# The FFN's output bias row: added onto each block of x by an accumulating DMA in place of a GpSimd operation

## Chip, cores and metric

The kernel runs on one core of a Trainium2 chip. The metric is device time in microseconds (us), the median of several runs. Before the change it is 741.25 us (3 runs, 739.79 to 741.45).

## What is computed

The input x has shape 8 x 1024 x 256. It passes through one attention layer and one feed-forward layer, each added onto its input and normalised afterwards. Cut to what matters:

```python
q, k, v = x @ Wq.T + bq, x @ Wk.T + bk, x @ Wv.T + bv      # 16 heads of 16
q, k = softmax(q, over the 16 of a head), softmax(k, over the 1024 rows)
state = einsum('bhnd,bhne->bhde', k, v)
out = einsum('bhnd,bhde->bhne', q, state)
x = layernorm(x + (layernorm(out) * ln_g + ln_b) @ Wo.T + bo)

h = layernorm(x) * ln1_g + ln1_b
h = gelu(h @ ternary(w1).T + b1)                           # 1024 hidden
h = layernorm(h) * ln2_g + ln2_b
x = layernorm(x + h @ ternary(w2).T + b2)
```

## The kernel before

**Tiling.** A batch of 1024 rows lies in SBUF as 128 partitions by 8 tiles by 256 columns (`xs[b]`). It is worked in two blocks of 4 tiles, 16 blocks in all; `x_of(i)` is the view of block i, 128 x 1024 numbers. x stays in SBUF and is updated in place: each block receives its attention result, is normalised, is read by the FFN, receives the FFN's result, is normalised again and is sent out.

**Attention.** The main loop (L781) goes over the 16 blocks and two more. For a block it makes keys (`keys`, L311, with `keys_exp`, L329, which takes running maxima, L333 and L335, and then the exponential, L338), queries (`queries_max`, L375, whose subtraction L378 is GpSimd's, and `queries_sum`, L385, with L391 on GpSimd), and the products of keys and x (`keys_x`, L407). Then a DMA issued from GpSimd's queue adds a row `crow` onto the block's x (L855). Two blocks later `attend` (L486) applies the state. A generator `norm` (L514) takes the statistics of a batch, adds the attention output to x (L526) and derives the scales, with the reciprocal square root in small steps of VectorE (`rsqrt`, L115 to L132). Its steps are handed out a few at a time by `more(n)` at fixed places of the loop, so VectorE's order is fixed when the kernel is built. The application of the scale (L772) is ScalarE's.

**FFN.** `ffn_slots` (L720) is a second generator, in slots of one column group; 8 slots make a block. Each slot makes one half of a hidden tile (`hidden`, L597, matmuls L615 and L619, gelu L620), turns hidden values (`turn`, L636, transposes L643, copies L568 on ScalarE and L569 on VectorE), and multiplies by the second weight matrix (`product`, L648, L657). Hidden work leads the products by 11 slots. Every eighth slot calls `enter` (L571) for the next block: GpSimd makes the scaled copy `h0` of x (L576), which is turned into the FFN's input (`turn_input`, L592), and then it adds the row `bout` onto x in place (L579). `bout` is a row of 256 numbers, the same in all partitions, made once from b2, ln2_b and w2 (L247). Later in the block's own 8 slots VectorE adds the part of the mean (`add_mean`, L680), then the FFN's result times its scale (`outputs`, L716), and takes statistics (`result_stats`, L686). One block later `finish` (L663) lets GpSimd scale and shift the four tiles (L670) and SP send them out (L673).

The FFN starts inside the attention loop: `enter(0)` runs at the last attention block but one, and three more calls of `enter` fall while the last attention blocks are still worked on. From block 4 on the FFN is alone. The order on each engine is that of the program (a manual schedule); semaphores between engines are set by the framework. An operation that reads or writes x waits for those before it that touch the same part.

**On GpSimd's queue**, therefore, stand in this order at each `enter`: the multiplication L576, the addition L579, and behind them whatever comes next: L378 and L391 of the next attention block with its L855, the next L576, or the four L670 of a finished block.

Of the kernel before, what the change touches and what calls it, by code (L numbers as in the profile page):

```python
# [12 lines left out]
ALU = mybir.AluOpType  # L13
AX = mybir.AxisListType

P = 128
# [6 lines left out]
def attn_ffn_postln_kernel(  # L23
# [11 lines left out]
    nc = tc.nc  # L35
    B, N, C = x.shape
# [6 lines left out]
    G = 4  # L43
# [96 lines left out]
    bout = const.tile([P, C], F32, name="bout")  # L140
# [152 lines left out]
    def x_of(i):  # L293
        b, g = blocks[i]
        return xs[b][:, g * G : (g + 1) * G, :]
# [275 lines left out]
    def enter(i):  # L571

        b, g = blocks[i]
        h0[i] = big.tile([P, G, C], F32, tag="h0", bufs=2, name=f"h0_{i}")
        rs2 = rs2_all[:, b * NT + g * G : b * NT + (g + 1) * G]
        nc.gpsimd.tensor_tensor(  # L576
            h0[i], x_of(i), rs2.unsqueeze(2).to_broadcast([P, G, C]), ALU.mult
        )
        nc.gpsimd.tensor_tensor(  # L579
            x_of(i), x_of(i), bout.unsqueeze(1).to_broadcast([P, G, C]), ALU.add  # L580
        )

    def turn_input(i, k):
# [136 lines left out]
    def ffn_slots():  # L720
        enter(0)
        yield
        turn_input(0, 0)
        turn_input(0, 1)
        for s in range(-LEAD, SLOTS):
            yield
            m = s + LEAD
            if m < SLOTS:
                if m % HC == 0 and m // HC + 1 < len(blocks):
                    enter(m // HC + 1)  # L730
                hidden(m)
                if m % HC in (5, 6) and m // HC + 1 < len(blocks):
                    turn_input(m // HC + 1, m % HC - 5)
            if 0 <= s + 2 < SLOTS:
                turn(s + 2)
            if m % 2 == 0 and 2 <= m < SLOTS + 2:
                squares((m - 2) // HC, (m - 2) % HC // 2)
            if s >= 0:
                norms(s)
                product(s)  # L740
                if s % HC == HC - 1:
                    outputs(s // HC)
        norms(SLOTS)
        norms(SLOTS + 1)
        last = len(blocks) - 1
        v = small.tile([P, 2 * NT], F32, tag="nv", name="nv_last")[:, :G]
        nc.vector.tensor_scalar(v, mv[last + 1][:, :G, 1], EPS, None, ALU.add)
        finish(last, mv[last + 1][:, :G, 0], finish_all(rsqrt(v, "last")))
# [167 lines left out]
```

## Time and profile before

| what | us |
|---|---|
| median of 3 runs | 741.25 (739.79 to 741.45) |
| profiled execution, its own time | 739.53 |
| span of its instructions | 737.8 |
| busy: TensorE matmuls | 690.7 (94% of the span) |
| busy: TensorE weight loads (beside matmuls) | 549.1 (74%) |
| busy: VectorE | 583.7 (79%) |
| busy: ScalarE | 441.0 (60%) |
| busy: GpSimd | 194.8 (26%) |

The profile is of one execution. PE is TensorE, PEld its weight loads, DVE VectorE, ACT ScalarE, POOL GpSimd, SP the engine that issues output DMAs. L579 is line 579 of the kernel; a group or a timeline line names line, engine, operation, what is written and read, the shape and the count; a bracket at its end tells how long the engine had been idle and who released it. In a timeline the first two numbers are start and duration in us. In the view of stretches a line gives the stretch, its length, busy time with the number of instructions for PE, PEld, DVE, ACT and POOL, then the clock granted to TensorE (1.00 is full), the DMA engines' share and GB/s. In the view of one source line durations are ns, as least, median and most. The page's mean clock over the span is 0.978.

### The profile page before, as it was taken

How to read it: one execution, taken by the hardware profiler on the slowest of the kernel's cores; microseconds unless marked ns; L12 is line 12 of the kernel's file. 1: busy time of each engine (PE TensorE's matmuls, PEld its weight loads, DVE VectorE, ACT ScalarE, POOL GpSimd, SP SyncE). 2: the span in 40 equal slices, each digit the busy share in tenths (PEclk: the TensorE clock that was granted, in tenths of full speed). 3: DMA queues.
4: the chain of work that ended last, by engine and by line, in shares of the span. 5: the costliest groups of instructions: out<-in, count | busy, mean ns of one | idle time of the engine just before them, and what ended most of it. 6: DMA issues, size and time to landing. Idle time of an engine off the chain costs nothing.

```text
span 737.8 us, 10770 instructions
## 1 busy us (share of the span) xinstructions
PE 690.7 (94%) x3780; PEld 549.1 (74%) x3780; DVE 583.7 (79%) x1642; ACT 441.0 (60%) x970; POOL 194.8 (26%) x156
## 2 busy tenths in 40 slices
PE   6899999979989999997998899999999999999992
PEld 4677766757657777765767788888888888888882
DVE  1667798877988959797898778877878877887686
ACT  2344436535364545546787667777777677677760
POOL 1232223121221222244420033332133333123112
PEclk9999999989999999998999899999999999999997
DMA  8833103222120111210100000000000000000001
GB/s 328 306 72 58 29 15 72 51 36 51 21 33 13 29 29 28 30 24 11 24 0 2 1 29 30 30 29 30 1 29 30 28 29 30 2 28 29 30 30 58
DMA packets 17238, 32.03 MB, mean 43 GB/s; under 512 B 1344, under 2 KB 12608, under 8 KB 16288
## 3 DMA queue, kind: packets, MB, share of 16 engines
q0 software_dynamic: 8608, 8.79, 7.9%
q1 hardware_dynamic: 7344, 21.50, 7.7%
q10 hardware_dynamic: 1232, 1.06, 0.4%
q8 instruction: 30, 0.49, 0.3%
q14 instruction: 24, 0.20, 0.1%
HBM read 14.56 MB, written 8.39 MB: 31 GB/s over the span
## 4 chain that ended last, share of the span: by engine, by line
PE 70%; DVE 23%; ACT 3%; DMA 2%; issue 2%; POOL 0%; POOLq 0%; ACTq 0%; DVEq 0%
PE pf L657 16%; PE ph L615 14%; PE pt L643 7%; PE po L498 6%; PE pq L364 5%; PE pa L407 5%; PE pk L322 5%; PE ph L619 3%; DVE x L526 3%; DVE st_y L532 2%; DMA wqkv_sb<-in_wqkv_dram 2%; PE pth L592 2%; PE ptq L301 1%; PE ptx L301 1%; DVE sto L508 1%
## 5 line engine op out<-in xcount | busy, mean ns | idle before, releaser
L657 PE MATMUL pf<-t,u 128*128 128x256 f32 x1024 | 157.5, 295 | 4.0 <-DVE x L716 3.6
L615 PE MATMUL ph<-t,hT 128*128 128x512 f32 x512 | 144.2, 403 | 1.2 <-DVE hT L569 1.2
L657 PEld LDWEIGHTS pf<-t,u 128*128 128x128 f32 x1024 | 131.9, 191 | 9.8 <-issue 5.8
L569 DVE SCALAR_TENSOR_TENSOR u<-pt,cols_sb,u 128x512 fp32r<-128x512 f32 x128 | 95.5, 746 | 45.6 <-ACT u L568 44.2
L620 ACT ACTIVATE h<-ph 128x512 f32<-128x512 f32 x128 | 76.5, 598 | 83.9 <-PE ph L619 73.7
L670 POOL TENSOR_SCALAR x<-x,ny_f,sh 128x256 f32<-128x256 f32 x60 | 38.1, 650 | 261.0 <-DVE sh L667 261.0
L615 PEld LDWEIGHTS ph<-t,hT 128*128 128x128 f32 x512 | 88.6, 189 | 15.3 <-DVE hT L569 1.9
L498 PE MATMUL po<-sm,qT 128*128 128x384 f32 x256 | 97.3, 505 | 0.1
L568 ACT ACTIVATE u<-pt,cols_sb 128x512 fp32r<-128x512 f32 x128 | 87.5, 684 | 8.3 <-PE pt L643 7.6
L643 PE MATMUL pt<-ident,h 128*128 128x128 f32 x512 | 78.1, 275 | 4.2 <-DVE u L569 2.5
L632 ACT ACTIVATE sq<-h,mvh 128x1024 f32<-128x1024 f32 x64 | 73.8, 1153 | 5.5 <-DVE mvh L624 5.5
L643 PEld LDWEIGHTS pt<-ident,h 128*128 128x128 f32 x512 | 61.6, 141 | 19.9 <-DVE hT L569 6.0
L378 POOL TENSOR_TENSOR q<-q,qm 128x1024 f32<-128x1024 f32 x16 | 30.8, 1926 | 150.1 <-DVE qm L377 90.6
L364 PE MATMUL pq<-wqkv_sb,xT 128*128 128x256 f32 x256 | 60.6, 380 | 0.8 <-DMA wqkv_sb<-in_wqkv_dram 0.8
L322 PE MATMUL pk<-xT,wqkv_sb 128*128 128x512 f32 x128 | 61.3, 603 | 0.0
L407 PE MATMUL pa<-x,ek 128*128 128x256 f32 x256 | 61.1, 382 | 0.0
L498 PEld LDWEIGHTS po<-sm,qT 128*128 128x128 f32 x256 | 46.5, 198 | 19.4 <-issue 2.1
L391 POOL TENSOR_TENSOR q<-q,rq 128x1024 f32<-128x1024 f32 x16 | 30.9, 1933 | 108.2 <-DVE rq L390 59.0
L407 PEld LDWEIGHTS pa<-x,ek 128*128 128x128 f32 x256 | 48.9, 192 | 13.1 <-issue 0.6
L364 PEld LDWEIGHTS pq<-wqkv_sb,xT 128*128 128x128 f32 x256 | 47.9, 190 | 12.7 <-issue 3.1
L680 DVE SCALAR_TENSOR_TENSOR x<-g2sum,ms,x 128x256 f32<-128x256 f32 x64 | 56.9, 927 | 0.0
L338 ACT ACTIVATE ekT<-pk,nb 128x512 f32<-128x512 f32 x32 | 21.7, 682 | 56.5 <-DVE nt_y L127 35.6
(144 smaller groups left out, 1151.9 us busy)
## 6 DMA issues: line engine op xcount, KB each, us to landing
x<-crow POOLq DMA_DIRECT2D x16, 512.0 KB, 5.5
out_dram<-x SPq DMA_DIRECT2D x16, 512.0 KB, 2.6
x<-in_x_dram SPq DMA_DIRECT2D x7, 1024.0 KB, 10.2
x<-in_x_dram SPq DMA_DIRECT2D x2, 512.0 KB, 5.6
wm_w<-in_w_dram SPq DMA_DIRECT2D x4, 256.0 KB, 8.0
wq_w<-in_w_dram SPq DMA_DIRECT2D x4, 256.0 KB, 2.5
wm_w<-in_w_dram SPq DMA_DIRECT2D x8, 128.0 KB, 2.1
wq_w<-in_w_dram SPq DMA_DIRECT2D x8, 128.0 KB, 2.0
```

The source lines that it names most:

```text
L322: nc.tensor.matmul(pk, wqkv_sb[:, k, C + c * P : C + (c + 1) * P], xT[i][:, k, :], start=(k == 0), stop=(k == KC - 1),)
L364: nc.tensor.matmul(pq[:, n, :], xT[i][:, k, (t + n) * P : (t + n + 1) * P], wqkv_sb[:, k, 0:C], start=(k == 0), stop=(k == KC - 1),)
L407: nc.tensor.matmul(pa[i][:, c, :], ek[i][:, t, c * P : (c + 1) * P], x_of(i)[:, t, :], start=(t == 0), stop=(t == G - 1),)
L498: nc.tensor.matmul(po[:, c * P : c * P + P + C], qT[i][:, c, t * P : (t + 1) * P], sm[b][:, c, :], start=(c == 0), stop=(c == KC - 1), ski ...
L568: nc.scalar.activation(hi, src, AF.Copy, scale=gain)
L569: nc.vector.scalar_tensor_tensor(lo, src, gain, hi.bitcast(F32), ALU.mult, ALU.subtract)
L615: nc.tensor.matmul(ph, hT[i][s][:, k, t * P : (t + 1) * P], t1[:, k, cols_j], start=(s == 0 and k == 0), stop=False,)
L620: nc.scalar.activation(h[i][t][:, cols_j], ph, AF.Gelu, accum_out=h[i, t][:, half : half + 1])
L632: nc.scalar.activation(sq, h[i][t], AF.Square, bias=mv[i][:, G + t, 0:1], accum_out=mv[i][:, G + t, 1:2])
L643: nc.tensor.transpose(pt[:, t * P : (t + 1) * P], h[i][t][:, j * P : (j + 1) * P], ident)
L657: nc.tensor.matmul(pf[i][t // 2][:, t % 2, :], u[s][:, n, t * P : (t + 1) * P], t2[:, j, :], start=(j == 0 and t % 2 == 0 and n == 0), sto ...
L680: nc.vector.scalar_tensor_tensor(x_t, g2sum, ms[i][:, t : t + 1], x_t, ALU.mult, ALU.add)
```

## The change

In `enter`, the GpSimd operation that adds `bout` onto the block is replaced by a DMA, issued from the same queue at the same place, that reads `bout` (repeated for the four tiles) and adds it onto x where x lies. Nothing else is changed.

```diff
         nc.gpsimd.tensor_tensor(
             h0[i], x_of(i), rs2.unsqueeze(2).to_broadcast([P, G, C]), ALU.mult
         )
-        nc.gpsimd.tensor_tensor(
-            x_of(i), x_of(i), bout.unsqueeze(1).to_broadcast([P, G, C]), ALU.add
+        nc.gpsimd.dma_start(
+            x_of(i), bout.unsqueeze(1).to_broadcast([P, G, C]), accum_op=ALU.add
         )
```

With it the waits change: the DMA waits for L576 on its own engine and for an earlier DMA that used the same semaphore; the first L680 of a block, its first L670 and its output DMA L673 now wait also for this DMA's landing. The order of instructions on every engine stays as it was.

## The prediction

> **What bounds the kernel now.** I looked first at what TensorE waits for in the pure FFN stage, 425 to 700 us, then at the operation that goes, then at every place where something near it is stretched. In the FFN stage TensorE waits for nobody: the view of waits is empty for it, and a stretch of 22 us, one block, is full. The line is stretch, length, then busy time of PE, weight loads, DVE, ACT and POOL.
>
> ```profile
> 512.00:534.00 22.00, 21.97 (x147) 19.27 (x146) 17.85 (x47) 15.95 (x35) 7.04 (x7) 1.00 0.07 26
> ```
>
> The operation is L579, 16 times, 2.46 us each. An accumulating DMA of the same shape is in the kernel already (L855, the row crow): 1.3 us on POOL, and the lines of the DMA view give 5.5 us to landing.
>
> ```profile
> L579 POOL TENSOR_TENSOR x<-x,bout x16: 2337/2463/2467, 330.9 to 669.4; 128x1024 f32<-128x1024 f32 x16
> L855 POOL DMA_DIRECT2D x<-crow x16: 1285/1298/1377, 30.1 to 347.9; - x16
> ```
>
> ```profile
> x<-crow POOLq DMA_DIRECT2D x16, 512.0 KB, 5.5
> ```
>
> Four of the 16 lie before 373 us, where attention and FFN overlap. There the timeline shows what L579 does to VectorE:
>
> ```profile
> 327.77 3.10 DVE L122 TENSOR_SCALAR ny_y<-nvy 128x16 int32<-128x16 int32 x1
> 328.39 2.44 POOL L576 TENSOR_TENSOR h<-x,rs_all 128x1024 f32<-128x1024 f32 x1
> ...
> 330.78 1.28 DVE L326 TENSOR_REDUCE mx<-pk 128x1 f32<-128x512 f32 x2
> 330.90 2.34 POOL L579 TENSOR_TENSOR x<-x,bout 128x1024 f32<-128x1024 f32 x1
> 332.09 1.17 DVE L333 TENSOR_TENSOR mb<-mx,bkv 128x2 f32<-128x2 f32 x1
> ...
> 333.55 0.69 ACT L338 ACTIVATE ekT<-pk,nb 128x512 f32<-128x512 f32 x1 [9.72 <-DVE nt_y L127]
> ...
> 334.38 0.47 PE L351 MATMUL pte<-ident,ekT 128*128 128x128 f32 x1 [3.50 <-ACT ekT L338]
> ```
>
> L333 writes two numbers a partition; its median is 161 ns, here it takes 1.17 us and ends at 333.26, when L579 ends (333.24). Likewise L122 ends with L576. Behind L333 wait the exponential of the keys and then TensorE, idle for 3.50 us. The chain of waits runs through exactly these: L122, L326, L333, L338, L351. The idle time has a second cost (the column before the DMA share is the granted clock):
>
> ```profile
> 331.00:333.00 2.00, 0.00 (x0) 0.00 (x0) 1.97 (x3) 0.00 (x0) 2.00 (x1) 1.00 0.94 134
> 333.00:334.00 1.00, 0.00 (x0) 0.00 (x0) 0.90 (x6) 0.45 (x1) 0.24 (x1) 0.98 0.00 0
> 334.00:340.00 6.00, 5.43 (x16) 3.80 (x17) 5.22 (x18) 3.45 (x11) 0.79 (x1) 0.50 0.00 1
> ```
>
> So TensorE works at half clock after the stall, until 340.8 us. A second run of stretched DVE steps:
>
> ```profile
> 352.42 1.19 DVE L519 TENSOR_SCALAR nvo<-mvo 128x8 f32<-128x8 f32 x1
> ...
> 353.64 1.82 DVE L122 TENSOR_SCALAR ny_o<-nvo 128x8 int32<-128x8 int32 x1
> 355.49 0.17 DVE L124 TENSOR_SCALAR ny_o<-ny_o 128x8 int32<-128x8 int32 x1
> 355.70 2.21 DVE L127 TENSOR_TENSOR nt_o<-ny_o 128x8 f32<-128x8 f32 x1
> 357.94 0.17 DVE L129 SCALAR_TENSOR_TENSOR nt_o<-nt_o,nvo 128x8 f32<-128x8 f32 x1
> ```
>
> POOL runs L579 from 351.20 to 353.57, L576 to 355.42, L579 from 355.50 to 357.88: L519, L122 and L127 each end with one of them.
>
> [...] The ends above agree to 0.04 us. During the issue of L855 at 288.54 us, L122 took 0.17 us: an issue alone did not hold it. [...] Half clock here lasts 6.83 us, two windows.
>
> **The change part by part.** The 16 L579 leave POOL; 16 issues of 1.3 us take their place in its queue, which keeps its order.
>
> At 330.9 us (block 0): L576 still ends at 330.83, so L122 keeps its 3.10 us. L333 starts at 332.09 and takes 0.16 instead of 1.17: 1.0 us less. The next operation on POOL comes only at 339.21[...]. L335, L338 and L351 follow, and TensorE's gap shrinks from 3.50 to 2.5 us. That is on the path: -1.0 us.
>
> The clock: by the trace, windows of 3.41 us in which TensorE was busy 0.10 to 0.32 of the time halved the clock, those at 0.49 and above did not (of 0.46 and 0.47 one of each). I lay such windows in every phase over a gap, close the gate where one is idle over 55%, and open it after a full busy one. A gap of 3.50 us then closes it in 93% of the phases and costs 2.0 us on average, 2.5 us in 63% and 1.2 us. The difference, about 0.85 us, is an estimate; in one execution it is 0 to 1.7. Bounds: at worst the restarted work falls wholly into half clock and 0.2 us are lost.
>
> At 351.2 us (blocks 1 and 2): the issue is followed at once by L576 of block 2, as L855 and L576 are at 347.89. That pair took until 351.12, 3.23 us; [...] from 351.2 to 354.4. L519 ends there, 0.9 us later than now, but L122 and L127 are free: L129 starts at 355.3 instead of 357.94, a lead of 2.6 us. The lead goes at two places. L624 at 358.62 needs ACT's accumulator, read out by 357.14, so 1.4 us remain; the L624 at 364.41 needs the one read out by 364.13, whose matmuls run on a TensorE without gaps: 0.2 us remain. At 368.41 L576 of block 3, which stays, blocks L526 as before, so TensorE's wait of 1.03 us at 371.24 stays too. I take -0.1 us; bounds 0 and -1.2 us (that wait and the 0.16 behind it).
>
> At 370.57 us (block 3) no DVE step is held by L579: 0.
>
> The other 12, every 21.9 us from 428.8 to 669.4: L579 stretches the second pair of L680 (3.14 us from 537.69, against 0.93 for the pair before). Up to 2.2 us of DVE time a block are freed, worth nothing: DVE afterwards waits for ACT's u (0.40 us) before the last L569 ahead of L716, and TensorE is never kept by the pair. If TensorE had slack, it would be worth at most 2.2 us a block.
>
> Added waits: the issue waits for L576 on its own engine, as L579 did, and for an old DMA on its semaphore, landed tens of us before. Behind it in POOL's queue are L378, L576 and L670; the issue is 1.1 us shorter than L579. The first L680 of a block, the first L670 and SP's output DMA wait for the landing. L680 of block 0 is at 398.99, 68 us after the issue, and 23 slots (63 us) follow for the others; 5.5 us are hidden. If the cover were gone, each block would pay 5.5 us. The last issue is 68 us before the end, so the tail is untouched.
>
> Sum: -1.0 - 0.1 - 0.85 = -1.95 us. The profiled execution took 739.53 us (span 737.8 and 1.7 around it), so 737.6; it lies 1.72 us under the median of the runs, 741.25, and from that I get 739.3.
>
> **The rivals.** Forecast, 0.50: 739.3; by the luck of the gate 738.4 to 740.2.
> The lead survives, 0.15: the steps between 352 and 372 take all of 1.2 us more: 741.25 - 3.15 = 738.1. For it speaks that DVE is busy 8.9 of 10 us there; against it the two waits for ACT and the L576 at 368.41.
> The gate gives nothing, 0.23: it falls as often and 0.2 us of the gain are lost: 741.25 - 1.1 + 0.2 = 740.35. For it: 2.5 us is still most of a window.
> Slower, 0.12: the 12 transfers in the stage that TensorE bounds slow its matmuls. A transfer of crow shows packets for 3.24 us; 12 make 38.9 us. Slowed by 5% they eat the 1.95 us; at 10% they cost 3.9 and the time is 743.2. For it: the four L615 within such a burst average 414 ns against 400 outside. Against it: L364, L322 and L498 have the same medians inside and outside bursts (379, 592, 486 ns), and L615's median too (395 and 396).
> That the change does not do what it says is excluded: the order of the instructions shows 16 copies of DMA in place of L579, and TensorE's and ACT's unchanged.
>
> **How the numbers follow.** What a measurement of this kernel can tell from no change is 0.2%, 1.5 us: 739.8. Of the forecast some 0.45 lies below it; with the second case 0.60. The third and the rest of the first are within, 0.28; slower 0.12. The low end, 737.2, is the second case with the gate's best luck (-1.1 - 1.2 - 1.7); the high end, 741.6, is past the third case by the scatter of the runs (741.45 at the highest). The slower case stays outside.
>
> **What would show it.** L333's longest near 0.16 us; TensorE's gap at 331 us about 2.5 us; less or no half clock after it; L127 at 0.17; L680's mean from 927 towards 550 ns; the wait before 371 us unchanged; a block still 21.9 us long. I am wrong if blocks lengthen, if L333 is still held[...], or if the gap at 371 closes.

## The result, and the profile after

The changed kernel takes 737.09 us (median of 22 runs, 734.84 to 739.95). The kernel before, run beside it on the same chip, takes 739.87 us (22 runs). The ratio is 0.9964 with a 95% interval of 0.9951 to 0.9977: 2.7 us less, between 1.7 and 3.6. The forecast was 739.3 us, 1.95 us below its median of before, 741.25 us; the ratio carried over to that median gives 738.6 us. What was gained is somewhat more than forecast, close to the rival "the lead survives" (3.15 us). The profiled execution took 737.86 us, with a span of 736.2.

In the view of one source line (least, median and most in ns) L333 is never held any more, L579 has become an issue of 1.3 us, and L680 has lost its long cases; its most was 2620 ns. The DMA view gives 5.5 us from issue to landing.

```profile
L333 DVE TENSOR_TENSOR mb<-mx,bkv x16: 160/160/163, 13.2 to 334.2; 128x2 f32<-128x2 f32 x16
```

```profile
L579 POOL DMA_DIRECT2D x<-bout x16: 1297/1304/1322, 333.2 to 667.8; - x16
```

```profile
L680 DVE SCALAR_TENSOR_TENSOR x<-g2sum,ms,x x64: 468/480/761, 396.9 to 723.5; 128x256 f32<-128x256 f32 x64
```

```profile
x<-bout POOLq DMA_DIRECT2D x16, 512.0 KB, 5.5
```

The timeline of the changed kernel at block 0:

```profile
329.83 3.10 DVE L122 TENSOR_SCALAR ny_y<-nvy 128x16 int32<-128x16 int32 x1
330.45 2.44 POOL L576 TENSOR_TENSOR h<-x,rs_all 128x1024 f32<-128x1024 f32 x1
...
333.19 1.31 POOL L579 DMA_DIRECT2D x<-bout  x1 [0.30 <-POOL h L576]
334.15 0.16 DVE L333 TENSOR_TENSOR mb<-mx,bkv 128x2 f32<-128x2 f32 x1
...
335.44 0.33 PE L351 MATMUL pte<-ident,ekT 128*128 128x128 f32 x1 [2.49 <-ACT ekT L338]
```

L122 is held by L576 exactly as long as before; L333, in the midst of the issue, is not; TensorE's gap is 2.49 us. The stretches after the gap (the clock is third from the end) still show half clock, but for one window of 3.41 us, where the profile of before had two:

```profile
335.40:336.70 1.30, 0.92 (x5) 0.72 (x6) 1.20 (x7) 0.66 (x2) 0.00 (x0) 1.00 1.20 173
336.70:340.10 3.40, 3.40 (x11) 2.20 (x10) 2.76 (x10) 2.07 (x7) 0.00 (x0) 0.51 0.52 76
340.10:342.00 1.90, 1.90 (x9) 1.34 (x9) 1.86 (x3) 1.08 (x3) 1.63 (x1) 0.98 0.00 0
```

A block of the FFN stage has TensorE as full as before, with VectorE 2 us less busy (15.85 us against 17.85):

```profile
512.00:534.00 22.00, 21.98 (x147) 19.20 (x146) 15.85 (x46) 15.77 (x36) 5.83 (x7) 1.00 0.22 48
```

The steps of the norm, from the timeline between 351 and 356 us. L519 alone is held, until L576 ends (2.28 us), and L129 follows at 355.29:

```profile
351.37 1.30 POOL L579 DMA_DIRECT2D x<-bout  x1 [0.30 <-POOL h L576]
352.19 2.41 POOL L576 TENSOR_TENSOR h<-x,rs_all 128x1024 f32<-128x1024 f32 x1
352.36 2.28 DVE L519 TENSOR_SCALAR nvo<-mvo 128x8 f32<-128x8 f32 x1
354.67 0.17 DVE L122 TENSOR_SCALAR ny_o<-nvo 128x8 int32<-128x8 int32 x1
...
355.09 0.17 DVE L127 TENSOR_TENSOR nt_o<-ny_o 128x8 f32<-128x8 f32 x1
355.29 0.17 DVE L129 SCALAR_TENSOR_TENSOR nt_o<-nt_o,nvo 128x8 f32<-128x8 f32 x1
```

Here the forecast fails. TensorE's wait at 371 us is gone. Before, the line was

```profile
372.27 0.50 PE L615 MATMUL ph<-t,hT 128*128 128x512 f32 x1 [1.03 <-DVE hT L569]
```

and no matmul of the changed kernel between 366 and 390 us waits.

**Where the 2.7 us come from.** To see it I set the start of every TensorE matmul in the profile after against the start of the same matmul in the profile before. The two executions already differ by +2.07 us when they reach 328 us, ahead of anything that was changed: 3.41 us of half clock from 22.72 us on, which the profile of before lacks, give +1.5 us, and half clock of 6.83 us in both, from 162.67 us on after and 159.88 us before, gives +0.6 us. From there on the difference moves like this:

| where (time in before) | step, us | what it is |
|---|---|---|
| 334 (L351) | -1.01 | the gap, 3.50 to 2.49 |
| 334 to 342 | -1.11 | half clock for 3.41 us in place of 6.83 |
| 361 | -0.37 | a wait of TensorE for y (L504), gone |
| 369 to 377 | -1.69 | the wait of 1.03 us for hT, its 0.16 us, and what followed |
| 409 to 426 | -0.4 | half clock at 409 us for 3.41 us in place of 6.83, at the same gap of 2.52 us: nothing near it was changed |
| 510 to 690 | +0.77 | 0.04 to 0.09 us a block, once 0.24 us |

The two profiled executions as a whole differ by only 1.67 us, since the 2.07 us of the start count against the change. Leaving out what the clock does, the steps are -1.01 - 0.37 - 1.69 + 0.77 = -2.3 us. So one item of the forecast is right, one much too small, and one was not in it at all: blocks of the FFN-only stage became longer.

### The profile page after: what moved, and what is told of

Its sections match the earlier page's. It is cut to its first block, busy times and chain, and to the rows that moved or that the text cites. A ratio compares the mean times of both kernels' runs of the same rounds, so it can differ in the third digit from the quotient of the medians.

```text
span 736.2 us, 10803 instructions
## 1 busy us (share of the span) xinstructions
PE 690.2 (94%) x3780; PEld 548.9 (75%) x3780; DVE 556.3 (76%) x1642; ACT 441.6 (60%) x970; POOL 177.0 (24%) x156
## 4 chain that ended last, share of the span: by engine, by line
PE 63%; DVE 19%; issue 9%; ACT 4%; DMA 3%; POOL 2%; ACTq 0%; POOLq 0%; DVEq 0%
PE ph L615 12%; PE pf L657 12%; PE po L498 7%; PE pt L643 5%; PE pa L407 5%; PE pq L364 5%; PE pk L322 5%; PE ph L619 3%; DMA wo_sb<-in_wo_dram 3%; DVE x L526 2%; DVE st_y L532 2%; POOL x L670 2%; PE ptq L301 1%; PE pth L592 1%; PE ptx L301 1%
## 5 line engine op out<-in xcount | busy, mean ns | idle before, releaser
L569 DVE SCALAR_TENSOR_TENSOR u<-pt,cols_sb,u 128x512 fp32r<-128x512 f32 x128 | 95.6, 747 | 66.0 <-ACT u L568 64.3
L615 PE MATMUL ph<-t,hT 128*128 128x512 f32 x512 | 143.7, 402 | 0.0
L620 ACT ACTIVATE h<-ph 128x512 f32<-128x512 f32 x128 | 76.6, 598 | 84.6 <-PE ph L619 74.3
L670 POOL TENSOR_SCALAR x<-x,ny_f,sh 128x256 f32<-128x256 f32 x60 | 38.5, 652 | 270.9 <-DVE sh L667 270.9
L615 PEld LDWEIGHTS ph<-t,hT 128*128 128x128 f32 x512 | 88.7, 189 | 13.6
L643 PE MATMUL pt<-ident,h 128*128 128x128 f32 x512 | 77.8, 274 | 4.7 <-DVE u L569 2.6
L643 PEld LDWEIGHTS pt<-ident,h 128*128 128x128 f32 x512 | 61.3, 140 | 21.2 <-DVE hT L569 7.0
L407 PE MATMUL pa<-x,ek 128*128 128x256 f32 x256 | 63.2, 392 | 0.0
L407 PEld LDWEIGHTS pa<-x,ek 128*128 128x128 f32 x256 | 50.5, 198 | 13.5 <-issue 0.6
L619 PE MATMUL ph<-brow,ones_r 128*128 128x512 f32 x128 | 50.7, 396 | 0.0
```

What stands on the lines that cost most here:

```text
L407: nc.tensor.matmul(pa[i][:, c, :], ek[i][:, t, c * P : (c + 1) * P], x_of(i)[:, t, :], start=(t == 0), stop=(t == G - 1),)
L569: nc.vector.scalar_tensor_tensor(lo, src, gain, hi.bitcast(F32), ALU.mult, ALU.subtract)
L615: nc.tensor.matmul(ph, hT[i][s][:, k, t * P : (t + 1) * P], t1[:, k, cols_j], start=(s == 0 and k == 0), stop=False,)
L619: nc.tensor.matmul(ph, ones_r, brow[:, cols_j], start=False, stop=True)
L620: nc.scalar.activation(h[i][t][:, cols_j], ph, AF.Gelu, accum_out=h[i, t][:, half : half + 1])
L643: nc.tensor.transpose(pt[:, t * P : (t + 1) * P], h[i][t][:, j * P : (j + 1) * P], ident)
```

## The experiments

Theory when I began: the first three DMAs give everything, through two separate places (block 0 through L333, blocks 1 and 2 through the norm's steps); the other twelve cost 0.8 us, because of a new wait on VectorE. Rivals: one place gives it all; the transfers themselves slow the blocks. All edits but that of "Later, with the GpSimd addition" are made in the changed kernel. "Before" is the kernel before on the same chip in the same series: 739.52 us (72 runs) for the first four, 739.56 (15) for the next four, 740.75 (11) for the rest.

### The DMA at block 0 alone

```diff
-        nc.gpsimd.dma_start(
-            x_of(i), bout.unsqueeze(1).to_broadcast([P, G, C]), accum_op=ALU.add
-        )
+        if i == 0:
+            nc.gpsimd.dma_start(
+                x_of(i), bout.unsqueeze(1).to_broadcast([P, G, C]), accum_op=ALU.add
+            )
+        else:
+            nc.gpsimd.tensor_tensor(
+                x_of(i), x_of(i), bout.unsqueeze(1).to_broadcast([P, G, C]), ALU.add
+            )
```

> Only block 0 is added by the DMA; the other 15 keep GpSimd's operation. Theory (L579 holds VectorE's steps in two places, each worth its own piece): L333 takes 0.16 us, TensorE's gap ahead of L351 (at 331 us before) is 2.5 us instead of 3.5, L127 in the stretch 352 to 358 us is still held (2.2 us), TensorE's wait for hT at 371 us is still 1.0 us, a lone FFN block lasts 21.87 us. Time against before: -1.0 us and 0 to -1.7 by the clock, so about -1.8. Rival (all of the gain hangs on the first gap, the rest follows from it): the wait at 371 us goes too and the time is about that of the full change, -2.8.

Measured: 738.97 us, ratio 0.9991 (0.998 to 1.0002). From its trace's timeline (lines after 579 stand five lower; L620 is L615):

```profile
333.46 0.16 DVE L333 TENSOR_TENSOR mb<-mx,bkv 128x2 f32<-128x2 f32 x1
...
334.75 0.33 PE L351 MATMUL pte<-ident,ekT 128*128 128x128 f32 x1 [2.50 <-ACT ekT L338]
...
354.95 2.21 DVE L127 TENSOR_TENSOR nt_o<-ny_o 128x8 f32<-128x8 f32 x1
...
371.52 0.49 PE L620 MATMUL ph<-t,hT 128*128 128x512 f32 x1 [1.02 <-DVE hT L569]
```

The gap shrinks, the norm's steps are held as ever, and the wait for hT stays. The trace confirms the place. The time is 0.5 us lower, 1.5 at most, and the interval just reaches no change at all: 1.0 us of gap fits, 1.0 and a whole gain of 0.85 us from the clock does not.

### The DMA at blocks 1 and 2 alone

The same edit with `if i in (1, 2):`.

> Only blocks 1 and 2 are added by the DMA. Theory: the gap at 331 us stays 3.5 us with half clock behind it; L122 and L127 behind L519 take 0.17 us; TensorE's wait at 371 us is gone, and its work at 375 us lies 2.0 us earlier against the work at 350 us; a lone FFN block 21.87 us. Time: -2.0 us. Rival (the first gap carries it all): the wait at 371 us stays and the time is unchanged within 0.3 us. The prediction's own step said -0.1 us here.

Measured: 738.38 us, ratio 0.9981 (0.997 to 0.9993). Timeline of this kernel:

```profile
336.19 1.17 DVE L333 TENSOR_TENSOR mb<-mx,bkv 128x2 f32<-128x2 f32 x1
...
338.48 0.48 PE L351 MATMUL pte<-ident,ekT 128*128 128x128 f32 x1 [3.50 <-ACT ekT L338]
...
354.99 2.27 DVE L519 TENSOR_SCALAR nvo<-mvo 128x8 f32<-128x8 f32 x1
357.30 0.17 DVE L122 TENSOR_SCALAR ny_o<-nvo 128x8 int32<-128x8 int32 x1
```

Here the gap stays and the wait for hT is gone: in the comparison of starts -0.36 and then -1.71 us. Hence the two places are separate, and the second is the larger one in the traces. By the times the gain is 1.1 us (0.5 to 2.2 by the interval); the 2 us expected are near its edge.

### The DMA from block 3 on

The same edit with `if i >= 3:`.

> Blocks 3 to 15 are added by the DMA, blocks 0 to 2 by GpSimd. Theory: nothing is gained; gap 3.5 us and wait at 371 us as before; a lone FFN block takes 21.93 instead of 21.87 us, because L122 now waits for GpSimd: together +0.8 us. Rival (GpSimd's load on VectorE costs time in the FFN stage as well): blocks shorter than 21.87 us and the time below before's by 1 us or more.

Measured: 740.35 us, ratio 1.0013 (1.0002 to 1.0023), 0.8 us more by the medians (0.1 to 1.7 by the interval), as expected. Gap 3.50 us, wait 1.03 us, both as before. The blocks from the eighth on last 21.94 us in place of 21.87 (from the first L592 of one to that of the next), one of them 22.13; the ten from the sixth on make 219.50 us against 218.72.

### The DMA at the first three blocks alone

The same edit with `if i < 3:`.

> Blocks 0 to 2 are added by the DMA, 3 to 15 by GpSimd. Theory: both gains and not the loss: gap 2.5 us, no wait at 371 us, a lone FFN block 21.87 us; time -3.0 us and 0 to -1.7 by the clock, so about -3.8, some 0.8 less than with all 16 by DMA. Rival (freeing VectorE in the FFN stage is worth something): slower than with all 16.

Measured: 736.68 us, ratio 0.9962 (0.9949 to 0.9975): 2.8 us less. The trace has the gap of 2.51 us, no wait for hT, and blocks of 21.87 us (the same ten: 218.71). By the trace this is the whole gain without the loss. By the times it can't be told from the full change (0.9964): 0.8 us lies within the two intervals.

### No addition at all

`enter` without the addition in all blocks, neither as an operation nor as a DMA, so the output lacks the row bout.

> The addition of the bias row is left out of all blocks: neither an operation nor a DMA (the output lacks it). Theory (the DMA itself costs the path nothing): the same TensorE gap as with the DMA, 2.5 us; no wait at 371 us; L519 is held only to the end of L576 of block 2, some 1.1 us after its start instead of 2.3; lone blocks 21.87 us, since L680 waits for GpSimd as before. Rival ([...]its transfer slows something): a gap clearly under 2.5 us or blocks under 21.8 us.

Measured: 735.01 us, one run. The gap is again 2.49 us, the wait for hT is gone, and blocks last 21.87 us. L519 takes 0.58 us, less than the 1.1 expected, against 2.28 with the DMA; yet in the comparison of starts the steps at 361 and 372 us are -0.36 and -1.72 us, as with the DMA. At block 0 and in the norm, then, the DMA costs TensorE nothing that shows. That it costs 0.07 us a block later is not the old GpSimd operation's absence, since that is absent here too.

### The DMA twice from block 4 on

```diff
-        nc.gpsimd.dma_start(
-            x_of(i), bout.unsqueeze(1).to_broadcast([P, G, C]), accum_op=ALU.add
-        )
+        for _ in range(2 if i >= 4 else 1):
+            nc.gpsimd.dma_start(
+                x_of(i), bout.unsqueeze(1).to_broadcast([P, G, C]), accum_op=ALU.add
+            )
```

The row is then added twice in those blocks.

> From block 4 on the DMA is issued twice (the bias row is added twice there). It keeps the waits of L122 for GpSimd. Theory (the wait lengthens the block, not the transfer): lone blocks from the eighth on 21.94 us, as with one transfer. Rival (transfers slow TensorE's matmuls): 22.01 us, twice the lengthening, and also the blocks ahead of the eighth longer than 21.87.

Measured: 735.71 us, one run; blocks from the eighth on 21.94 us, the ten from the sixth on 219.48 (the changed kernel: 219.43). Twice the bytes and twice the issues add nothing to a block, so the transfers don't lengthen it. This takes away the mechanism of the prediction's slower case.

### Another reader's buffer, so that the new wait falls elsewhere

The order of VectorE's instructions with their waits shows what changed in a block. Before:

```
L122 TensorScalarPtr ny_f_6769<-nv_f_6766 128x8 [waits DVE_49]
L680 TensorScalarPtr x_82<-g2sum,ms_6825,x_82 128x256 [waits DVE_49,Pool_49]
```

After:

```
L122 TensorScalarPtr ny_f_6769<-nv_f_6766 128x8 [waits DVE_49,Pool_49]
L680 TensorScalarPtr x_82<-g2sum,ms_6825,x_82 128x256 [waits DMASW7_49,DVE_49]
```

`ny_f`, written by L122, lies in a buffer whose former contents GpSimd's L670 read as its scale. VectorE must know that this L670 is done. Before, an earlier L680 had already waited for a later GpSimd operation (L579), which covered it. Now L680 waits for the DMA, and the wait for GpSimd appears on L122, though L670 was done long ago. The list of waits under "The change" lacks this one. In the changed kernel's trace it is an instruction of its own ahead of L122; this is a line of the view of source line L122, and that view of the kernel before has no such line:

```profile
L122 DVEq EVENT_SEMAPHORE  x12: 21/21/21, 505.5 to 727.9; - x12
```

The kernel with the DMA from block 3 on has it too, those with the first three DMAs alone or with no addition don't. The experiment gives L670 a copy of the scale, made on VectorE behind L667:

```diff
+        rsc = small.tile([P, G], F32, tag="rsc", name=f"rsc_{i}")
+        nc.vector.tensor_copy(rsc, rs)
...
-                x_t, x_t, rs[:, t : t + 1], sh[:, t : t + 1], ALU.mult, ALU.add
+                x_t, x_t, rsc[:, t : t + 1], sh[:, t : t + 1], ALU.mult, ALU.add
```

> All 16 by DMA, and VectorE copies the four scales into a tile of their own behind L667, which GpSimd's L670 reads in place of ny_f; L122 then has no wait for GpSimd any more, the transfers stay. Theory: lone blocks 21.87 us, the time 0.8 us under that with 16 DMAs: about -3.3 us against before. Rival (the transfers lengthen the block): 21.94 us, no change against 16 DMAs.

Measured: 735.94 us, ratio 0.9956 (0.994 to 0.9973), 3.3 us less; by the times this can't be told from the changed kernel, by the blocks it can: they last 21.83 to 21.87 us (the same ten: 218.53). The wait is not gone. It stands twelve times ahead of L667, which writes the tile of the shift that L670 reads as well:

```profile
L667 DVEq EVENT_SEMAPHORE  x12: 21/21/21, 509.0 to 730.4; - x12
```

In the changed kernel's timeline one block looks like this:

```profile
593.27 0.17 DVE L700 TENSOR_SCALAR nv_f<-mvh 128x4 f32<-128x4 f32 x1
593.54 0.17 DVE L122 TENSOR_SCALAR ny_f<-nv_f 128x8 int32<-128x8 int32 x1
...
596.44 0.42 PEld L643 LDWEIGHTS pt<-ident,h 128*128 128x128 f32 x4 [0.34 <-DVE hT L569]
```

and with the copy (L702 is L700):

```profile
593.96 0.16 DVE L702 TENSOR_SCALAR nv_f<-mvh 128x4 f32<-128x4 f32 x1
594.15 0.17 DVE L122 TENSOR_SCALAR ny_f<-nv_f 128x8 int32<-128x8 int32 x1
...
597.05 0.42 PEld L643 LDWEIGHTS pt<-ident,h 128*128 128x128 f32 x4 [0.28 <-DVE hT L569]
```

From L700 to L122 it is 0.27 us with the wait and 0.19 without. VectorE is behind here, and L643 waits for its L569, 0.34 us, against 0.28 with the copy and also in the kernel before. Those 0.06 us are the longer block. L670 had ended some 15 us before L122; it is the wait's being there that costs, not anything waited for, and it costs the block only where it stands: L122 comes before the L569 that L643 waits for, L667 after it. The block with 0.24 us (22.11 us long, always at the same place) shows L124 waiting 0.22 us for L122; it is gone with the copy too, but why that one costs three times as much stays open.

### The first call of enter one attention block later

After these runs one stall of 2.5 us was left at block 0, and it came from L576, which the change doesn't touch. Here the call is moved to the next attention block, behind `queries_max`:

```diff
+        if i == len(blocks) - 1:
+            for _ in prep:
+                pass
+            next(slots)
...
-        if i == len(blocks) - 2:
-            for _ in prep:
-                pass
-            next(slots)
```

> All 16 by DMA; the call of enter for block 0 comes after the queries' maximum of the last attention block, so that L576 of block 0 stands behind L378 in GpSimd's queue and no longer beside L122. Theory (what is left of TensorE's gap, 2.5 us, is L122 held by that L576): L122 takes 0.17 us, the gap ahead of L351 is under 0.5 us and no half clock follows it: -2.5 - 1.7 = about -4 us against the full change, -6.5 against before. The steps L431 and L508 near 342 us are held by L576 instead, with slack. Rival (the gap is bound by something else, or L576 does the same harm in its new place): gap 2 us or more, or a new wait of TensorE between 340 and 350 us; time as the full change.

Measured: 733.12 us, ratio 0.9912 (0.989 to 0.9935), 6.5 us less. Timeline of this kernel:

```profile
331.18 0.18 DVE L122 TENSOR_SCALAR ny_y<-nvy 128x16 int32<-128x16 int32 x1
...
332.58 0.16 DVE L333 TENSOR_TENSOR mb<-mx,bkv 128x2 f32<-128x2 f32 x1
...
334.13 0.96 PE L351 MATMUL pte<-ident,ekT 128*128 128x128 f32 x4
```

L351 has no bracket: TensorE does not wait, and no half clock follows. The kernel's 3.5 us gap was thus L576 and L579 of block 0, 2.5 and 1.0 us of it. In its new place L576 costs little: between 343 and 350 us 0.16 us are lost in the comparison of starts. The blocks from the eighth on still last 21.93 us, since the wait on L122 is still there.

### Both: later, and with the copy

> The DMA at all 16 places, with the first call of enter moved to the next attention block (as in the run before) and a VectorE copy of rs in finish (as in the run before that). If the two costs are separate and add up: -6.5 us for the move and -0.8 us for the shorter blocks, so 7.3 us less than the kernel before (ratio 0.990); no wait of TensorE ahead of L351, no stretch of half clock near 335 us, blocks from the 8th on 21.87 us. If the copy only puts the wait of VectorE on another instruction that TensorE waits for as well: -6.5 us, blocks 21.93.

Measured: 731.83 us (731.42 to 734.07), ratio 0.9892 (0.9877 to 0.9908), 8.0 us less, the fastest kernel of this study. The stretch that held gap and half clock is now nearly full, at clock 1.00:

```profile
330.00:342.00 12.00, 11.62 (x54) 8.38 (x52) 10.87 (x35) 8.64 (x23) 5.25 (x5) 1.00 0.30 44
```

The ten blocks from the sixth on make 218.58 us, with the wait at L667 again, so by the trace the two edits add up; the time agrees (7.3 us expected).

### Later, with the GpSimd addition

The same move of the call in the kernel before.

> The GpSimd addition L579 kept at all places, only the first call of enter moved to the next attention block. My theory: moving takes the collision with L122 and L333 away with or without the DMA, so the gap of 3.5 us ahead of L351 and the half clock after it go (about -5 us by 342 us). But GpSimd's queue then holds L576 and L579 of block 0 ahead of L391 and the row crow, 1.1 us more than with the issue, and behind them L579, L576 and L579 stretch the steps L519, L122, L127 as before, so the wait of TensorE near 371 us stays or grows: about -4.5 us against the kernel before, 2 us less than the same move with the DMA. Blocks 21.87 us. Rival: the DMA gives nothing once the call is moved; then -6.5 to -7.3 us.

Measured: 736.06 us, ratio 0.9943 (0.9929 to 0.9958), 4.2 us less. Timeline of this kernel:

```profile
355.22 2.38 POOL L579 TENSOR_TENSOR x<-x,bout 128x1024 f32<-128x1024 f32 x1
355.40 2.23 DVE L131 SCALAR_TENSOR_TENSOR ny_o<-nt_o,ny_o 128x8 f32<-128x8 f32 x1
...
358.19 1.15 ACT L632 ACTIVATE sq<-h,mvh 128x1024 f32<-128x1024 f32 x1 [3.42 <-DVE mvh L624]
...
360.01 1.56 PE L498 MATMUL po<-sm,qT 128*128 128x384 f32 x4 [1.79 <-ACT y L504]
...
371.59 0.49 PE L615 MATMUL ph<-t,hT 128*128 128x512 f32 x1 [1.01 <-DVE hT L569]
```

The gap at block 0 is gone without the DMA. But L579 then holds the norm's steps, L624 comes late, ScalarE waits for it, and TensorE for ScalarE: 1.79 us, and the old wait for hT behind it. By the comparison of starts the DMA is worth 3.8 us in this order (from 328 to 388 us the kernel with move, DMA and copy gains 8.7, this one 4.8); the medians differ by 4.2 us. Without the copy, the move and the DMA gained 6.5 us, 2.3 more than the move alone. The rival had the move alone at -6.5 to -7.3 us and is out.

### Two GpSimd operations on a tile that nobody else uses

```diff
+    spare = const.tile([P, 2, C], F32, name="spare")
+    nc.gpsimd.memset(spare, 0.0)
...
+        if i == 0:
+            for _ in range(2):
+                nc.gpsimd.tensor_tensor(
+                    spare, spare, bout.unsqueeze(1).to_broadcast([P, 2, C]), ALU.add
+                )
         nc.gpsimd.dma_start(
```

> The changed kernel with two extra GpSimd additions of 128 x 512 onto a spare tile between L576 and the DMA of block 0, some 2.4 us in all, which touch nothing that VectorE or TensorE use. If L333 was held [...]not by the data of x: L333 is held again, about 1.1 us, and the gap ahead of L351 is back at about 3.5 us. If it was held by the data or by the order of the semaphores: L333 0.16 us and a gap of 2.5 us, as in the changed kernel. One look, so only the trace is read.

One run (L335, L353 and L578 are L333, L351 and L576):

```profile
329.59 4.31 DVE L122 TENSOR_SCALAR ny_y<-nvy 128x16 int32<-128x16 int32 x1
330.21 2.44 POOL L578 TENSOR_TENSOR h<-x,rs_all 128x1024 f32<-128x1024 f32 x1
...
332.06 3.14 POOL L583 TENSOR_TENSOR spare<-spare,bout 128x512 f32<-128x512 f32 x2
...
335.13 0.16 DVE L335 TENSOR_TENSOR mb<-mx,bkv 128x2 f32<-128x2 f32 x1
...
336.41 0.33 PE L353 MATMUL pte<-ident,ekT 128*128 128x128 f32 x1 [3.70 <-ACT ekT L340]
```

The gap is back, 3.70 us, though nothing in these operations touches x, L122 or L333. It was not the data, then: a GpSimd operation held a VectorE step with which it shares no tile, L122 for 4.31 us in place of 3.10. How it does so, no run shows. My expectation had the wrong victim: L122 is held, through L576 and the first of the two, to 333.90, and L333 comes too late to meet the second. That L333 itself was held in the same way before is inferred from its end, which is that of L579 to 0.02 us.

## Why the prediction was right or wrong

**The gap at block 0** (-1.0): right, to 0.01 us, L333 (0.16 us) and L122 (3.10 us) as forecast, and the experiment with block 0 alone shows it by itself. L122 starts 0.62 us ahead of L576 (329.83 and 330.45 us; before, 327.77 and 328.39) and yet ends with it, to 0.04 us; why it is held from so early on was not shown.

**The norm's steps, L519 to L129**: right. L129 came 2.65 us earlier, against 2.6 forecast, and the pair of issue and L576 took 3.2 us; L519 ended 0.2 us later than I had put it.

**"The lead goes at two places ... I take -0.1 us"**: this is the step that failed. It measured -0.37 - 1.69 = -2.06 us. I had said that the L624 at 364.41 needs the accumulator read out at 364.13, leaving 0.2 us of the lead. But a hidden tile has two halves, and L624 runs once both are done; that L624 belonged to the L620 at 361.06, read out at 361.77 (before):

```profile
361.54 0.23 ACT L620 ACTIVATION_READ_ACCUMULATOR h<-ph 128x1 f32 x1
...
364.41 0.20 DVE L624 TENSOR_SCALAR mvh<-total 128x1 f32<-128x1 f32 x1
```

The L624 at 358.62 was misread in the same way: it needed the half read out at 355.43, not at 357.14, and came 2.65 us earlier, so that the lead was not cut there either. In the changed kernel the second L624 runs ahead of the next half:

```profile
360.13 0.60 ACT L620 ACTIVATE h<-ph 128x512 f32<-128x512 f32 x1 [0.51 <-PE ph L619]
360.62 0.19 ACT L620 ACTIVATION_READ_ACCUMULATOR h<-ph 128x1 f32 x1
...
362.51 0.20 DVE L624 TENSOR_SCALAR mvh<-total 128x1 f32<-128x1 f32 x1
363.02 0.60 ACT L620 ACTIVATE h<-ph 128x512 f32<-128x512 f32 x1
...
367.83 0.45 DVE L526 SCALAR_TENSOR_TENSOR x<-y,ny_o,x 128x256 f32<-128x256 f32 x1
...
368.00 2.04 POOL L576 TENSOR_TENSOR h<-x,rs_all 128x1024 f32<-128x1024 f32 x1 [11.81 <-PE pth L592]
...
368.98 1.40 DVE L569 SCALAR_TENSOR_TENSOR hT<-pth,gs,hT 128x512 fp32r<-128x512 f32 x2
```

So 1.9 us of the lead are kept, the last L526 starts ahead of L576 of block 3, which I had said would block it (before, it took 1.03 us there), and the L569 of hT starts at 368.98 instead of 371.47, 2.5 us sooner. The rival "the lead survives" had the mechanism, but its bound of 1.2 us was too small as well: it counted the wait of 1.03 us and the 0.16 behind it, not the matmuls behind those nor the wait at 361 us.

**The clock** (-0.85): not borne out. The step that failed is "in every phase", an assumption of my estimate that no trace had shown. What the trace had shown of single windows held. In the profiles of before and after, the starts and ends of half clock between 15 and 700 us lie whole multiples of 3.41 us apart, and each half clock lasts 3.41 or 6.83 us. I laid windows of 3.41 us from the starts of half clock over the stretch from 15 to 700 us of all 13 traces. At full clock, windows in which TensorE was busy for 0.44 of the time or less were followed by half clock, those with 0.50 or more were not, and from 0.46 to 0.49 there were both. In those two profiles half clock ended after each of its windows in which TensorE was busy for 0.93 or more (nine) and went on after those with 0.82 or less (four). But the gap did not fall in any phase. In the six traces where it was 2.5 us long it began between 0.38 us before and 0.19 us after the start of a window, so that the window was busy for 0.17 to 0.28 only. Why the phases lie so close together stays open. In all five further traces with a gap of 2.5 us at this place the clock was halved, for 3.41 us each time, as it was in the profile after; with 3.5 to 3.7 us it was halved for 3.41 us in three and for 6.83 us in one. So the -1.11 us between the compared profiles come from the 6.83 us of the one profile of before; what the clock adds to the medians can't be split off: 2.7 us measured, of which 2.3 by the steps without the clock. The rival "the gate gives nothing" was right on the clock and wrong on the time, for the reason above. Only taking the gap away altogether spared the half clock, in three traces of three.

**The twelve later blocks** (0): wrong by +0.77 us, and on the side that I had not looked at. I went through the waits that the DMA adds, not through the waits that the removed operation had covered. I named the L680 that now waits for the landing, but not that it no longer waits for GpSimd, so that L122 must. And "TensorE waits for nobody" held for its matmuls alone: from 425 to 700 us of the kernel before its weight loads waited twelve times for VectorE, L643 for L569, 3.5 us in all (4.1 in the changed kernel). That is where a later VectorE lengthens the block.

**Hidden landing, an issue that does not hold L333, no transfer cost**: right. The landing took 5.5 us, and ahead of no L680 of the changed kernel did VectorE stand idle; L333 took 0.16 us in the midst of the issue. The runs with no addition (blocks of 21.87 us) and with two DMAs (21.94 us, as with one) show the last; the slower case had no ground.

So the norm's lead was under-estimated by 2.0 us and the blocks by 0.8 us in the other direction, and the 0.85 us credited to the clock can't be found: that the sum came nearer than its parts is luck. Two of the signs that I had named for being wrong did come: blocks lengthened, and the wait at 371 us closed.

## What to carry to other kernels

Where a GpSimd operation stretches small VectorE steps (here L333, 1.17 us in place of 0.16), look at what TensorE waits for behind them; there an accumulating DMA was worth having, and elsewhere it wasn't (three of sixteen gave all of the gain, 2.8 us; the other thirteen alone took 0.8 us more). When an operation goes, list the waits that waiting for it had covered: each may come back on a later instruction, where here it cost 0.06 us a block ahead of what TensorE waits for, and nothing behind it. And before an edit shortens a stall, see whether the call that causes it can be moved: by the medians moving one call gave more than the change (4.2 us against 2.7, and 6.5 for both), though the intervals of the first two overlap.

## What the runs showed that I had not expected

- A wait on a semaphore that was set long ago, added to a VectorE step of 0.17 us, made it start 0.06 to 0.08 us later, and each block paid it, because TensorE's weight loads waited at that place for VectorE. The same wait 3.4 us further on, behind what TensorE waits for, cost nothing (blocks of 21.83 to 21.87 us).
- A VectorE step that is held isn't always let go between two GpSimd operations: L122 was held through L576 and the first spare operation (4.31 us), but only through L576 where L579 followed it on the same x (3.10 us). Sharing data is not the whole of it: in the kernel before L519 was let go at 353.61, between L579 and an L576 that works on another block. What decides it was not tried.
- A gap of 2.5 us of TensorE, less than one clock window of 3.41 us, cost half clock for a whole window in six traces of six, each time beginning close to the start of a window.
